# One hand-written order for the stages ahead of the typed projection in a graph, mixing and MoE kernel

## The chip, the cores and the metric

The kernel runs on one core of a Trainium2 chip. Its engines are TensorE (PE, with PEld for the loading of weights), VectorE (DVE), ScalarE (ACT), GpSimd (POOL) and SyncE (SP), each with an instruction queue of its own that it works through in order. DMAs are issued from the queues of SP, ACT and POOL; indirect DMAs (a gather or scatter of rows by a list of indices) from POOL's. The metric is the device time of one execution in microseconds (us), lower is better. Profile and timed runs are separate executions.

## What is computed

N = 3125 nodes with 256 features, E = 103125 edges sorted by receiver (`dst`), 19 node types, and a mixture of 16 experts. Everything is float32. Cut to what matters:

```python
xn = layernorm(x)                                       # per node
# graph part: linear maps by node type, attention over edges, both directions
K, Q, V = (typed_linear(xn, W, b, node_type) for W, b in ((Wk, bk), (Wq, bq), (Wv, bv)))
e0, e1, e2 = (cos(log(t + 1) * w_time + b_time) for t in edge_attr[:, :3].T)
att, v = edge_msgs(K[row], Q[col], V[row], e1, e2)      # 4 heads
agg = segment_sum([v * segment_softmax(att, col), e0], col) + the same with row and col exchanged
g = layernorm(typed_linear([agg, agg], Wa, ba) + xn) * gamma[node_type] + beta[node_type]
# mix part: linear attention over all nodes, 8 heads
q, k = elu(xn @ wq + bq) + 1, elu(xn @ wk + bk) + 1;  vm = xn @ wv + bv
kv, k_sum = sum over nodes of k^T vm, and of k
mix = ((q @ kv) / (q . k_sum + 1e-6)) @ wo + bo
x = x + g + mix
# MoE: 16 experts, the best 2 for each node, two-layer networks with relu
out = x + layernorm(xl + moe(xl)) * gamma2 + beta2      # xl = layernorm(x)
```

Since `q.sum` over heads is all that the graph attention needs of Q, the four 56-wide parts of Wq are added together ("folded") to one before the projection.

## The kernel before

Nodes lie in NT = 25 tiles of 128 rows (the last has 53). The stages ahead of the edges ("the head") are these; line numbers are those of the profile.

- **Rows of the edge list.** The receivers (`idx`, 128 x 808 and one more) are turned to float (`nf`) and written to `ends` in DRAM, 512 rows of 202. For each node tile one VectorE instruction (L391) counts how many of the 512 first entries lie below the node, which gives the row its edges begin in (`row_i`); POOL gathers that row for each of the 128 nodes (`er`, L357, one indirect DMA a tile, six buffers), and a second instruction (L401) counts within it. Both together give `start`, the place of the node's first edge, and by differences `deg`, how many it has.
- **Types' sort** (`sorted_rows`, L293 and around): a place for each node in a list sorted by type, with each type padded to whole tiles, JS = 43 of them; `stype` is that place.
- **Norms** (L424 to L430): moments by tile, a square root for each group of six tiles, then `XN` (normalised rows), whose two halves are transposed by TensorE (`pt`, L285) and copied to `XNT` by ACT (L286). POOL scatters each tile of `XN` to `xbuf` in the order of types (L351, 25 scatters, each `issue_after` the last gather of `er`).
- **Receivers' sort** (L439 to L492): nodes sorted by their number of edges, so that blocks of 128 have about the same. A matrix `pick` (25 x 64 flags a partition), running sums (`running`, L292 and L293), ranks by matmuls (L487, L488), then `place_i`. POOL scatters 25 tiles of records to `order` (L351) and loads them back as `ordt` (L555).
- **Edges** (L500 to L517): in four parts, load senders and three times, ACT takes logarithms, and a store writes records to `recs`.
- **Weights**: SP loads b, Wk, Wv, and Wq type by type (19 pieces of two loads, two buffers `wq`); VectorE folds each (L527 to L529).
- **Attention's sums** (L573 to L591): for each tile keys and values, `ps_kv` = two matmuls of 128 x 512 over `XNT`; VectorE adds biases (`k` L576, `low` L578, `v` L581), ACT takes an exponential (L579), VectorE ends `k` (L583), and TensorE adds k^T v over all tiles in `acc` (L585). The masked result is `state`.

The order of all this is not the text's: a scheduler places the instructions of the head on each engine by their readiness and its own costs. From the projection on the order is written by hand (`tc.manual_schedule()`): for each of the JS tiles `load_tile` (SP), `turn_tile`, `project` (TensorE L726; VectorE adds the bias into `prow`, L734, three buffers), pieces of the mix part (`mix`, with `queries` for four tiles at a time, L768 to L773, which need `XNT`, and `mixes`, which need `state`), and `place`, which has POOL copy the places (L739) and scatter the projected rows to `table` (L740). At tile 8 `ordered()` reads `ordt`, and the lists of edges are then worked off between tiles. Edge blocks, output and MoE follow.

The pools of the head lie on a stack: `ep` (side right) until the end of the attention's sums, `normed` (XN) inside it until the receivers' sort is done, `wqp` for the Wq pieces, and `mixs` (k, low, v) on the room that `normed` gave back.

Of the kernel before, what the change touches and what calls it, by code (L numbers as in the profile page):

```python
# [97 lines left out]
def gnn_mix_moe_kernel(ctx: ExitStack, tc: tile.TileContext, a, out):  # L98
# [97 lines left out]
    e2 = right.enter_context(tc.tile_pool(name="eprep2", bufs=2, side="right"))  # L196
# [19 lines left out]
    turned = first.enter_context(tc.tile_pool(name="turned", bufs=1))  # L216
    normed = ExitStack()
# [18 lines left out]
    for i, k in enumerate(("wq", "wk", "wv")):  # L236
        nc.sync.dma_start(wqkv[:, :, i, :], a[f"L0_mix_{k}"].rearrange("(c p) o -> p c o", p=P))
    wo = mw.tile([P, 2, D], F32, name="wo")
    nc.sync.dma_start(wo, a["L0_mix_wo"].rearrange("(c p) o -> p c o", p=P))
# [7 lines left out]
    nc.vector.tensor_scalar(bq1, bqc, 1.0, None, op0=OP.add)  # L247
# [8 lines left out]

    zp = first.enter_context(tc.tile_pool(name="zero", bufs=1))
    none = ep.tile([P, ROW], F32, name="none")
    nc.gpsimd.memset(none, -1.0)
# [3 lines left out]
    scales = zp.tile([T, 2, DZ], F32, name="scales")  # L263
# [4 lines left out]
    bo = zp.tile([T, D], F32, name="bo")  # L268
    src = a["L0_mix_bo"]
    nc.gpsimd.dma_start(bo, bass.AP(tensor=src.tensor, offset=src.offset, ap=[[0, T], [1, D]]))  # L270
    nc.vector.tensor_tensor(scales[:, 1, :D], scales[:, 1, :D], bo, OP.add)
# [4 lines left out]

    wp = first.enter_context(tc.tile_pool(name="wproj", bufs=1))
    w = wp.tile([P, T, 2, WC], F32, name="w")
# [17 lines left out]

    def sorted_rows(gp, ps_r, pick, K, J):

# [7 lines left out]
        nc.tensor.matmul(total.rearrange("p t e -> p (t e)"), ones, pv, start=True, stop=True)  # L306
        run = gp.tile([P, NT + 1, K], F32, name="run0")
# [59 lines left out]

    nf = ep.tile([P, EW + 1], F32, name="nf")
    nc.vector.tensor_copy(nf, idx)
    kept_ends = nc.gpsimd.dma_start(ends.rearrange("(p r) t -> p (r t)", p=P), nf[:, :EW]).ins  # L370
    with tc.issue_after(kept_ends):
        nc.sync.dma_start(xbuf.rearrange("(t p) d -> p t d", p=P), bc(blank, 1, JS + 1))
    down = ep.tile([P, EW], F32, name="down")
    nc.vector.tensor_tensor(down, nf[:, :EW], nf[:, 1:], OP.is_gt)
    nc.vector.tensor_reduce(bad[:, 0:1], down, AX.X, OP.max)


    ps = ps_c.tile([P, LR, P], F32, name="ps_first")
    for r in range(LR):
        nc.tensor.transpose(ps[:, r, :], nf[:, r * ET:r * ET + 1].to_broadcast([P, P]), ident)  # L380
    firsts = ep.tile([P, LR * P], F32, name="firsts")
    nc.scalar.copy(firsts, ps.rearrange("p r q -> p (r q)"))
    node_i = ep.tile([P, NT], I32, name="node_i")
    nc.gpsimd.iota(node_i, pattern=[[P, NT]], base=0, channel_multiplier=1)
    rec = ep.tile([P, NT, 4], F32, name="rec")
    node = rec[:, :, 0]
    nc.vector.tensor_copy(node, node_i)
    row = ep.tile([P, NT], F32, name="row")
    for t in range(NT):
        junk = e2.tile([P, max(ET, LR * P)], F32, name="junk", bufs=1)  # L390
        nc.vector.tensor_scalar(junk[:, :LR * P], firsts, node[:, t:t + 1], 0.0, op0=OP.is_lt, op1=OP.add,  # L391
                                accum_out=row[:, t:t + 1])
    nc.vector.tensor_scalar(row, row, -1.0, 0.0, op0=OP.add, op1=OP.max)
    row_i = ep.tile([P, NT], I32, name="row_i")
    nc.vector.tensor_copy(row_i, row)
    within = ep.tile([P, NT], F32, name="within")
    for t in range(NT):
        er = e2.tile([P, ET], F32, name="er", bufs=6)
        counted = gather_rows(er, ends, row_i[:, t:t + 1]).ins
# [20 lines left out]
    with tc.tile_pool(name="ps_t", bufs=2, space=PSUM) as ps_t:  # L420
        for g0, gn in groups:
# [7 lines left out]
            for t in range(g0, g0 + gn):  # L429
# [3 lines left out]
                with tc.issue_after(counted):  # L433
                    scatter_rows(xbuf, stype[:, t:t + 1], XN[:, t, :], "xrows")
# [1298 lines left out]
```

## Time and profile before

| What | us |
|---|---|
| median of 3 timed runs (2707.68 to 2709.11) | 2709.07 |
| the profiled execution, and its span | 2717.76, 2716.0 |
| start of the first projection matmul (L726) | 237.44 |
| er gathers, xbuf scatters, order scatters (POOL) | 52.4 to 86.7, 87.0 to 118.7, 155.1 to 187.1 |
| counts of rows (L391) | 25.7 to 51.1 |
| norms (L430), first and last start | 20.1 and 104.6 |
| first k (L576), last matmul into acc (L585) | 140.4, 227.7 |
| state done, ordt's load issued | 228.6, 190.5 |

The profiled execution is 0.3% above the median of the timed runs. Times in the text are from the start of its span. In lists of groups each row has the busy time, the mean in ns of one, and after the second bar how long the engine stood idle just before these instructions and who released it ("issue": nothing that the profile shows; "remote": a source that it doesn't know). A window row has the busy time and count of PE, PEld, DVE, ACT and POOL in turn, then the TensorE clock that was granted (1 is full), the share of DMA time and GB/s. In the timeline a row has its start, its duration, the engine (a trailing q: its queue, which issues DMAs), line, operation, tiles and, in brackets, the idle time before it.

### The profile page before, as it was taken

How to read it: one execution, taken by the hardware profiler on the slowest of the kernel's cores; microseconds unless marked ns; L12 is line 12 of the kernel's file. 1: busy time of each engine (PE TensorE's matmuls, PEld its weight loads, DVE VectorE, ACT ScalarE, POOL GpSimd, SP SyncE). 2: the span in 40 equal slices, each digit the busy share in tenths (PEclk: the TensorE clock that was granted, in tenths of full speed). 3: DMA queues.
4: the chain of work that ended last, by engine and by line, in shares of the span. 5: the costliest groups of instructions: out<-in, count | busy, mean ns of one | idle time of the engine just before them, and what ended most of it. 6: DMA issues, size and time to landing. Idle time of an engine off the chain costs nothing. (4 is left out here: it accounts for less than half of the span.)

```text
span 2716.0 us, 28309 instructions
## 1 busy us (share of the span) xinstructions
PE 2084.6 (77%) x7139; PEld 1274.6 (47%) x7139; DVE 1918.1 (71%) x3769; ACT 1230.2 (45%) x3019; POOL 1497.5 (55%) x1525
## 2 busy tenths in 40 slices
PE   2268665278898898989988888898877853599994
PEld 1034342134555455555554554455554541377773
DVE  7465777377889899999999998999972463122226
ACT  1112222265666666666666566657632350133332
POOL 3531468776777777777777776766613614222210
PEclk7579787677989898999899899898986755699997
DMA  9434567896667666666666766666636561255554
GB/s 282 137 77 129 165 194 226 286 314 183 181 202 202 177 192 192 195 197 193 190 198 202 199 187 178 192 182 188 178 124 204 174 197 66 99 174 173 174 156 146
DMA packets 236151, 496.03 MB, mean 183 GB/s; under 512 B 31509, under 2 KB 148340, under 8 KB 235476
## 3 DMA queue, kind: packets, MB, share of 16 engines
q0 software_dynamic: 88480, 325.71, 40.2%
q1 hardware_dynamic: 139428, 158.87, 20.0%
q10 hardware_dynamic: 8080, 9.59, 1.2%
q8 instruction: 63, 1.03, 0.1%
q14 instruction: 100, 0.82, 0.1%
HBM read 415.68 MB, written 78.37 MB: 182 GB/s over the span
## 5 line engine op out<-in xcount | busy, mean ns | idle before, releaser
L357 POOL DMA_INDIRECT rowt<-table,idx x854 | 999.8, 1171 | 394.6 <-issue 231.3
L1394 PE MATMUL pl<-rowt,ident 128*128 128x448 f32 (+2 forms) x944 | 496.9, 681 | 100.5 <-issue 55.3
L1394 PEld LDWEIGHTS pl<-rowt,ident 128*128 128x128 f32 x944 | 210.3, 234 | 382.2 <-issue 283.8
L1446 PE MATMUL pa<-keep,ident 128*128 128x256 f32 x1708 | 380.6, 380 | 7.0 <-DVE keep L1444 7.0
L1446 PEld LDWEIGHTS pa<-keep,ident 128*128 128x128 f32 x1708 | 325.7, 191 | 73.5 <-issue 27.7
L1359 PE MATMUL ps_u<-wide,turned 49*128 49x448 f32 (+2 forms) x708 | 323.2, 592 | 47.9 <-ACT turned L1352 27.0
L1338 DVE TENSOR_TENSOR rowt<-rowt 128x1260 f32<-128x1260 f32 (+2 forms) x118 | 178.4, 1512 | 140.4 <-DMA rowt<-table,idx 61.7
L1328 ACT ACTIVATE rowt<-rowt,KT 128x60 f32<-128x60 f32 x854 | 216.2, 334 | 20.9 <-DMA rowt<-table,idx 20.0
L1359 PEld LDWEIGHTS ps_u<-wide,turned 49*128 49x128 f32 x708 | 128.0, 194 | 189.7 <-issue 126.0
L351 POOL DMA_INDIRECT ybuf<-y,to_i x64 | 61.4, 960 | 265.0 <-DVE y L1169 224.0
L1352 ACT COPY turned<-pt 42x128 f32<-42x128 f32 (+2 forms) x118 | 30.6, 259 | 386.6 <-PE pt L1350 218.3
L1387 DVE TENSOR_TENSOR rowt<-rowt,qq 128x672 f32<-128x672 f32 (+2 forms) x236 | 197.7, 878 | 4.0
L1361 ACT ACTIVATE half<-ps_u 128x448 f32<-128x448 f32 (+2 forms) x354 | 190.9, 539 | 2.2 <-remote 1.1
L1161 ACT ACTIVATE hT<-ps_h,b 128x128 f32<-128x128 f32 x256 | 94.1, 368 | 213.2 <-PE ps_h L1160 211.5
L1160 PE MATMUL ps_h<-zT,w 128*128 128x128 f32 x1024 | 180.1, 295 | 12.6 <-ACT hT L1161 10.0
L1339 DVE TENSOR_REDUCE KT<-rowt 128x21 f32<-128x1260 f32 (+2 forms) x118 | 178.3, 1511 | 4.1
L1160 PEld LDWEIGHTS ps_h<-zT,w 128*128 128x128 f32 x1024 | 149.8, 192 | 58.2 <-ACT hT L1161 44.0
L1440 DVE TENSOR_TENSOR keep<-keep,both 128x1176 f32<-128x1176 f32 (+2 forms) x118 | 167.0, 1416 | 0.0
L1355 ACT COPY keep<-rowt 128x1344 f32<-128x1344 f32 (+2 forms) x118 | 159.1, 1348 | 13.3 <-PE pa L1446 13.3
L1165 PE MATMUL ps_e<-w,hT 128*128 x512 | 157.6, 390 | 0.0
L1373 PE MATMUL pe<-te,ident 128*128 128x256 f32 x472 | 117.1, 371 | 34.9 <-ACT te L1362 24.4
L1362 ACT ACTIVATE te<-half 128x448 f32<-128x448 f32 (+2 forms) x236 | 139.1, 590 | 7.8 <-ACT half L1361 0.3
(374 smaller groups left out, 3375.6 us busy)
## 6 DMA issues: line engine op xcount, KB each, us to landing
w<-in_L_ffn_w_dram SPq DMA_DIRECT2D x80, 512.0 KB
rowt<-table,idx POOLq DMA_INDIRECT x854
h<-in_L_gnn_Wa_dram SPq DMA_DIRECT2D x19, 512.0 KB
bias<-bbuf SPq DMA_DIRECT2D x43, 220.0 KB
zbuf<-zero SPq DMA_DIRECT2D x1, 8514.0 KB
zr<-zbuf SPq DMA_DIRECT2D x64, 129.0 KB
yb<-ybuf SPq DMA_DIRECT2D x16, 384.0 KB
xbuf<-blank SPq DMA_DIRECT2D x1, 5654.0 KB
```

The costliest lines, as they stand in the source:

```text
L357: return nc.gpsimd.indirect_dma_start(out=dst, out_offset=None, in_=buf[:, :], in_offset=IndirectOffsetOnAxis(ap=idx, axis=0))
L1160: nc.tensor.matmul(ps[:, f, :], w1[:, c, f * P:(f + 1) * P], zT[:, c, :], start=(c == 0), stop=(c == 1))
L1328: nc.scalar.activation(key[:, s, :], key[:, s, :], AF.Square, bias=chk[q]["b"]["k"][:, s0 + s, 1:2])
L1338: nc.vector.tensor_tensor(times, times, bc(rowt[:, :n, :CAP], 2, 3), OP.mult)
L1339: nc.vector.tensor_reduce(b["times"][:, s0:s1, 1::2], times, AX.X, OP.add)
L1355: nc.scalar.copy(keep[:, :n, :PROJ], rowt[:, :n, VC:QC])
L1359: nc.tensor.matmul(ps[:, :n * 2 * TD], lT, wide[:, k, :n * 2 * TD], start=True, stop=True)
L1361: nc.scalar.activation(half[:, :n, :].rearrange("p s j -> p (s j)"), ps[:, :n * 2 * TD], AF.Sin)
L1387: nc.vector.tensor_tensor(to, kt, bc(qq[:, :n, d, :], 2, 3), OP.mult)
L1394: nc.tensor.matmul(pl[:, :n], ident, part[:, :, :, a, :], start=(a == 0), stop=(a == PARTS - 1))
L1440: nc.vector.tensor_tensor(v3, v3, bc(b["both"][:, s0:s1, :3], 3, DK), OP.mult)
L1446: nc.tensor.matmul(b["pa"], ident, keep[:, s, :], start=(s0 + s == 0), stop=(s0 + s == c - 1))
```

## The change

The whole head is put under `tc.manual_schedule()`, so each engine now runs its instructions in the order of the text, and the text is rewritten to that end:

- Order: moments of the first group, `nf`, the types' `pick` and its matmuls, then all 25 row counts one after the other (`rows_of_edges`, called from inside `sorted_rows`), the first six gathers of `er`, the rest of the types' sort, the fold of b, all other moments and one square root for all tiles, edges 0 and 1. Then one loop over the 25 tiles: the gather for tile t+6, norm and transposes of t, the count within for t, and after every second tile from the fourth one `keys()`. `keys()` begins a tile of the attention's sums (`keys_of`) and ends the one before (`sum_keys`).
- Behind the loop come the 25 xbuf scatters, edges 2 and 3, and the receivers' sort as a generator, `order_rows`, cut into 14 steps, with a `keys()` behind the work of each step and one fold behind every third. Then the 25 order scatters, `ordt`, the last folds, `state` and the checks on the edge order (`down`) and times (`top`).
- Wq comes in five pieces of up to four types, and a fold is three instructions for all types of its piece.
- Each xbuf and order scatter takes its indices from a copy made by POOL (`apart`, three buffers).
- Queues: bk, bv and bq are loaded on POOL's queue, edges 0 and 1 on SP's, `gbuf` and `bbuf` stored on ACT's; Wk and Wv follow the fill of `xbuf` on SP, which no longer waits until `ends` is issued.
- Pools: `mixs` is open from the start, so the sums over keys need no room from `XN`; `early` (zq: edges, biases, and what is written first) closes before `late` (Wq pieces, receivers' sort) opens in its place; one PSUM tile `ps_c` serves three uses, and `pr` has two buffers.

What is removed is the same work in the text of before, printed above; of the new text, the lines that the prediction speaks of:

```diff
-    none = ep.tile([P, ROW], F32, name="none")
-    nc.gpsimd.memset(none, -1.0)
...
+    early = ExitStack()
+    zq = early.enter_context(tc.tile_pool(name="early", bufs=2))
+    none = zq.tile([P, ROW], F32, name="none", bufs=1)
...
-    nc.vector.tensor_tensor(scales[:, 1, :D], scales[:, 1, :D], bo, OP.add)
+    nc.gpsimd.dma_start(b[:, :PROJ], a["L0_gnn_bk"])
+    nc.gpsimd.dma_start(b[:, PROJ:2 * PROJ], a["L0_gnn_bv"])
+    bq = zq.tile([T, PROJ], F32, name="bq", bufs=1)
+    nc.gpsimd.dma_start(bq, a["L0_gnn_bq"])
...
-    for q in range(4):
-        ri = e2.tile([P, QT], I32, name="ri")
-        raw = e2.tile([P, QT, 5], F32, name="raw")
+    edges, kept_er = {}, {}
...
+    def load_edges(q, eng):
+        ri = zq.tile([P, QT], I32, name="ri")
+        raw = zq.tile([P, QT, 5], F32, name="raw")
...
+        load_rows(eng, ri, a["src"], E, EW, q * QT, (q + 1) * QT)
+        load_rows(eng, raw.rearrange("p t c -> p (t c)"), a["edge_attr_5"], 5 * E, 5 * EW, 5 * q * QT, 5 * (q + 1) * QT)
+        edges[q] = ri, raw
...
+    def keep_edges(q):
+        ri, raw = edges.pop(q)
+        rc = zq.tile([P, QT, 4], F32, name="rc")
...
         nc.scalar.dma_start(recs[:P * EW, :].rearrange("(p t) c -> p t c", t=EW)[:, q * QT:(q + 1) * QT, :], rc)
...
+    def apart(idx, side):
+        at = ep.tile([P, 1], I32, name=f"at_{side}", bufs=3)
+        nc.gpsimd.tensor_copy(at, idx)
+        return at
...
+    with tc.manual_schedule():
+        for i, k in enumerate(("w_time", "b_time")):
+            s = a[f"L0_gnn_{k}"]
+            nc.scalar.dma_start(wb[:, i, :], bass.AP(tensor=s.tensor, offset=s.offset, ap=[[0, P], [1, TD]]))
+        for q in range(2):
+            load_edges(q, nc.sync)
+        for i, k in enumerate(("wq", "wk", "wv")):
+            nc.sync.dma_start(wqkv[:, :, i, :], a[f"L0_mix_{k}"].rearrange("(c p) o -> p c o", p=P))
+        nc.sync.dma_start(wo, a["L0_mix_wo"].rearrange("(c p) o -> p c o", p=P))
+        nc.sync.dma_start(xbuf.rearrange("(t p) d -> p t d", p=P), bc(blank, 1, JS + 1))
+        load_w(w[:, :, :, :PROJ], a["L0_gnn_Wk"], nc.sync)
+        load_w(w[:, :, :, PROJ:2 * PROJ], a["L0_gnn_Wv"], nc.sync)
+        node_i = ep.tile([P, NT], I32, name="node_i")
+        nc.gpsimd.iota(node_i, pattern=[[P, NT]], base=0, channel_multiplier=1)
+        moments_of(0)
...
+        nc.vector.tensor_copy(nf, idx)
+        nc.gpsimd.dma_start(ends.rearrange("(p r) t -> p (r t)", p=P), nf[:, :EW])
...
+        nc.scalar.copy(firsts, ps.rearrange("p r q -> p (r q)"))
+        with tc.tile_pool(name="sort", bufs=1, side="right") as gp, tc.tile_pool(name="ps_r", bufs=1, space=PSUM) as ps_r:
...
+            def rows_of_edges():
+                nc.vector.tensor_copy(node, node_i)
+                for t in range(NT):
+                    junk = er_p.tile([P, max(ET, LR * P)], F32, name="junk", bufs=1)
+                    nc.vector.tensor_scalar(junk[:, :LR * P], firsts, node[:, t:t + 1], 0.0, op0=OP.is_lt, op1=OP.add,
+                                            accum_out=row[:, t:t + 1])
+                nc.vector.tensor_scalar(row, row, -1.0, 0.0, op0=OP.add, op1=OP.max)
+                nc.vector.tensor_copy(row_i, row)
+            base, own = sorted_rows(gp, ps_r, pick, T, JS, rows_of_edges)
...
+            for t in range(6):
+                kept_er[t] = er_p.tile([P, ET], F32, name="er")
+                gather_rows(kept_er[t], ends, row_i[:, t:t + 1])
...
+        nc.vector.tensor_tensor(scales[:, 1, :D], scales[:, 1, :D], bo, OP.add)
+        fold(b[:, 2 * PROJ:], bq)
+        nc.scalar.dma_start(gbuf, scales.rearrange("t i d -> t (i d)"))
+        nc.scalar.dma_start(bbuf, b)
+        for g in range(1, len(groups)):
+            moments_of(g)
...
+        nc.scalar.activation(rs, mv[:, :, 1], AF.Sqrt, bias=eps_c)
...
+        def keys_of(t):
+            ps = ps_kv.tile([P, 512], F32, name="ps_kv")
+            for c in range(2):
...
+        def sum_keys(t):
+            k, low, v = made.pop(t)
+            n = rows[t]
+            nc.vector.scalar_tensor_tensor(k, k, 1.0, low, op0=OP.add, op1=OP.max)
+            for c in range(2):
...
+        n_keys = [0]
+        def keys():
+            t = n_keys[0]
+            n_keys[0] += 1
+            if t < NTR:
+                keys_of(t)
+            if 0 < t <= NTR:
+                sum_keys(t - 1)
...
+        keep_edges(0)
+        load_edges(2, nc.scalar)
+        keep_edges(1)
+        load_edges(3, nc.scalar)
+        with tc.tile_pool(name="ps_t", bufs=2, space=PSUM, side="right") as ps_t:
+            for t in range(NT):
+                if t + 6 < NT:
+                    kept_er[t + 6] = er_p.tile([P, ET], F32, name="er")
+                    gather_rows(kept_er[t + 6], ends, row_i[:, t + 6:t + 7])
+                nc.vector.tensor_scalar(XN[:, t, :D], XN[:, t, :D], mv[:, t, 0:1], rs[:, t:t + 1],
+                                        op0=OP.subtract, op1=OP.mult)
+                transposed(XNT[:, :, t * P:(t + 1) * P], XN[:, t, :D], ps_t, "pt")
+                junk = er_p.tile([P, max(ET, LR * P)], F32, name="junk", bufs=1)
+                nc.vector.tensor_scalar(junk[:, :ET], kept_er.pop(t), node[:, t:t + 1], 0.0, op0=OP.is_lt, op1=OP.add,
+                                        accum_out=within[:, t:t + 1])
+                if t % 2 == 1 and t > 2:
+                    keys()
+        for t in range(NT):
+            scatter_rows(xbuf, apart(stype[:, t:t + 1], "x"), XN[:, t, :], "xrows")
+        normed.close()
+        for q in range(2, 4):
+            keep_edges(q)
+        early.close()
...
+        late = ExitStack()
+        gp = late.enter_context(tc.tile_pool(name="dsort", bufs=1))
+        wqp = late.enter_context(tc.tile_pool(name="wq", bufs=2))
+        step = 4
+        folds = []
+        for k in range(0, T, step):
+            n = min(step, T - k)
+            folds.append((k, n))
+        wqs = {}
+        def load_fold(i):
+            k, n = folds[i]
+            wqs[i] = wqp.tile([P, step, 2, PROJ], F32, name="wq")
+            load_w(wqs[i][:, :n], a["L0_gnn_Wq"][k:k + n], nc.sync)
+        def fold_one(i):
+            k, n = folds[i]
+            fold(w[:, k:k + n, :, 2 * PROJ:].rearrange("p t c o -> p (t c) o"),
+                 wqs.pop(i)[:, :n].rearrange("p t c o -> p (t c) o"))
+            if i + 2 < len(folds):
+                load_fold(i + 2)
+        for i in range(2):
+            load_fold(i)
...
+        def order_rows():
+            start = ep.tile([P, NT + 1], F32, name="start")
...
+            nc.tensor.matmul(ps, shift[:, 1, :], start[:, 1:], start=False, stop=True)
+            yield
...
+            dst, at = gp.tile([P, NT + 1, K], F32, name="run"), 1
+            while at <= NT:
+                nc.vector.tensor_copy(dst[:, :at], run[:, :at])
+                nc.vector.tensor_tensor(dst[:, at:], run[:, at:], run[:, :NT + 1 - at], OP.add)
+                run, dst, at = dst, run, 2 * at
+                yield
...
+        with tc.tile_pool(name="ps_d", bufs=2, space=PSUM, side="right") as ps_d:
+            steps = order_rows()
+            i = 0
+            for s, _ in enumerate(steps):
+                if n_keys[0] <= NTR:
+                    keys()
+                if s % 3 == 2 and i < len(folds):
+                    fold_one(i)
+                    i += 1
+        for t in range(NT):
+            scatter_rows(order, apart(place_i[:, t:t + 1], "o"), rec[:, t, :], "order")
+        nc.gpsimd.dma_start(ordt, order.rearrange("(t p) c -> p t c", p=P))
+        while n_keys[0] <= NTR:
+            keys()
+        while i < len(folds):
+            fold_one(i)
+            i += 1
...
+        down = nf[:, 1:]
+        nc.vector.tensor_tensor(idx[:, :EW], nf[:, :EW], down, OP.is_gt)
+        nc.vector.tensor_reduce(row_i[:, 0:1], idx[:, :EW], AX.X, OP.max)
...
+        mix_ps.close()
+        late.close()
+        right.close()
```

## The prediction

> **What bounds the kernel now.** I read the page first (span 2716.0 us; TensorE busy 77%, but in the first four slices 2, 2, 6, 8 tenths with the clock at 7, 5, 7, 9), because the change touches only what lies before the projection. Then the windows of that head, up to the first projection matmul (L726) at 237.44 us:
>
> ```profile
> core 0: us, PE busy (x) PEld busy (x) DVE busy (x) ACT busy (x) POOL busy (x), PEclk, DMA share, GB/s
> 0.00:42.00 42.00, 11.92 (x28) 5.77 (x28) 30.46 (x118) 8.74 (x14) 8.98 (x26) 0.88 0.98 276
> 42.00:100.00 58.00, 11.23 (x34) 4.94 (x34) 32.73 (x134) 7.42 (x21) 33.93 (x36) 0.52 0.79 227
> 100.00:140.00 40.00, 10.57 (x18) 4.40 (x18) 19.75 (x49) 5.76 (x10) 14.39 (x15) 0.50 0.35 115
> 140.00:200.00 60.00, 39.17 (x109) 19.11 (x109) 35.00 (x138) 8.25 (x17) 26.34 (x26) 0.80 0.32 65
> 200.00:237.00 37.00, 31.62 (x109) 15.72 (x107) 20.77 (x60) 7.00 (x18) 0.00 (x0) 0.91 0.20 52
> ```
>
> No engine fills the head: VectorE works 139 of 237 us, TensorE 105, POOL 84. It is a chain of waits. Which ones, the groups of instructions in 20 to 237 us show:
>
> ```profile
> L573 PE MATMUL ps_kv<-wqkv,XNT 128*128 128x512 f32 x100 | 53.8, 660 | 2.2 <-DVE v L581 1.4 <-DVE w L529 0.7
> L351 POOL DMA_INDIRECT order<-rec,place_i x25 | 24.7, 989 | 43.7 <-DVE w L527 36.4 <-issue 7.3
> L351 POOL DMA_INDIRECT xbuf<-XN,stype x25 | 24.4, 975 | 7.6 <-issue 7.0 <-DVE run L292 0.3 <-DMA xbuf<-XN,stype 0.3
> L391 DVE TENSOR_SCALAR_CACHE_REDUCE junk<-firsts,rec 128x512 f32<-128x512 f32 x25 | 18.4, 735 | 0.0
> L430 DVE TENSOR_SCALAR XN<-XN,mv_x,r_x 128x256 f32<-128x256 f32 x25 | 10.6, 434 | 3.2 <-remote 3.2
> L576 DVE TENSOR_TENSOR k<-ps_kv,bkv 128x256 f32<-128x256 f32 x25 | 10.6, 423 | 25.6 <-remote 20.1 <-PE ps_kv L573 5.1 <-issue 0.5
> L401 DVE TENSOR_SCALAR_CACHE_REDUCE junk<-er,rec 128x202 f32<-128x202 f32 x25 | 10.5, 419 | 20.2 <-DMA er<-ends,row_i 6.3 <-DVE XN L430 5.0 <-remote 4.9
> L527 DVE TENSOR_TENSOR w<-wq 128x112 f32<-128x112 f32 x19 | 5.1, 270 | 0.9 <-issue 0.5 <-DMA wq<-in_L_gnn_Wq_dram 0.5
> L487 PE MATMUL pr<-pick,before 128*128 128x512 f32 (+1 forms) x8 | 5.6, 796 | 5.7 <-DVE pick L470 4.1 <-DVE at L490 1.6
> L488 PE MATMUL pr<-run,ones 128*128 128x512 f32 (+1 forms) x8 | 4.5, 652 | 10.0 <-DVE run L292 10.0
> ```
>
> The reader should see that the sums over keys (L573 to L585) begin only after 140 us (first k at 140.4) although the norms (L430) are done at 104.6, and that POOL's three trains of 25 indirect DMAs (52 to 87, 87 to 119, 155 to 187 us) stand one behind the other. Last, SP's queue and the end of the head in the timeline:
>
> ```profile
> 22.96 0.37 SPq L372 DMA_DIRECT2D xbuf<-blank  x1
> 23.98 17.62 SPq L532 DMA_DIRECT2D b<-in_L_gnn_bk_dram  x1
> 53.53 13.28 SPq L523 DMA_DIRECT2D w<-in_L_gnn_Wv_dram  x2
> 66.86 9.26 SPq L523 DMA_DIRECT2D wq<-in_L_gnn_Wq_dram  x4
> ...
> 230.82 3.78 PE L768 MATMUL ps_q<-XNT,wqkv 128*128 128x512 f32 x4 [2.81 <-DVE qT L773]
> 237.44 1.74 PE L726 MATMUL ps<-w,xT 128*128 x4 [0.57 <-issue]
> ```
>
> The DMA engines are full until about 80 us, and a transfer behind them holds its queue: the 14 KB load of b took 17.62 us to issue.
>
> **The change, term by term.** All times are from the span's start. Code after the first projection tile is the same, so what counts is when that stage starts and how freely it runs.
>
> 1. *Start of the tile loop: 72 us.* Counts (25 x 0.735 = 18.4 us), types' sort (some 11) and the moments of 19 tiles (19 x 0.40) run back to back from about 19, so VectorE could be at the norms by 57. But ACT's queue now holds, ahead of its first XNT copy, the loads of edges 2 and 3 and the store of edges 1, and by the built program their issues wait for completion slots that the xbuf fill, Wk and Wv used last. So ACT, in order, stands until Wv has landed; each transpose's PSUM tile waits behind it, and VectorE behind that (its reduction over edges 1 needs ACT's logarithms). Bytes up to there: x 3.2, dst 0.4, edges 0 and 1 1.4, mix weights 1.05, xbuf fill 5.8, Wk and Wv 7.5, small ones 1.3: 20.6 MB. The first 15 us moved 238 GB/s = 3.6 MB; the other 17 MB at 297 GB/s (window 15 to 42) take 57 us: 72. Bounds: 57 (nothing held) and 76 (SP through with its last full-queue issue in before).
>
> 2. *Loop: 63 us.* Four tiles alone (4 x 1.5), then 11 pairs, each with one keys(). TensorE in order: two transposed tiles 2 x 0.38, ps_kv 1.88, acc 0.61 (full clock); acc waits for k, low, v, k, 0.42 + 0.31 + 0.42 + 0.42 = 1.57 us on VectorE: 4.8, with the XNT copy (0.37) 5.2. 11 x 5.2 = 57. Bounds: VectorE alone, 2 x (0.41 + 0.50) + 1.57 = 3.4 each; half clock (ps_kv 3.78, as L768 shows for this shape) 7.9. I take 5.2: TensorE is busy 3.25 of 5.2 us, nearest to the window 140 to 200 (39.2 of 60, clock 0.80), not to 42 to 140 (21.8 of 98, clock 0.5). End 135. The er gathers, now issued six ahead of the counts, have 15 us each and cost nothing; if the loop were faster than 1.26 us a tile, their pace in before, they would set it.
>
> 3. *Edges 2 and 3: 5.6 us.* ACT table load 1.28, two sets of logarithms 2 x 1.77, a reduction 0.77; nothing lies beside it on VectorE: 141.
>
> 4. *Fourteen steps: 67 us.* Each has a keys(): 1.57 on VectorE, then acc + next ps_kv, 0.61 + 1.88, beside which the step's own VectorE work lies: sort about 22 us and folds. The folds were 19 x (0.27 + 0.27 + 0.20) = 14 us and become five of four types; by a 128x440 add of 0.62 (L734) that is 5 x (0.62 + 0.62 + 0.35) = 8. 30/14 = 2.1 fits under 2.49. So 14 x 4.06 = 57, and the ranks' matmuls in TensorE's order 5.6 + 4.5 = 10. End 208. Bounds: 54 (VectorE alone, 22 + 24 + 8) and 102 (half clock, 14 x 6.6 + 10).
>
> 5. *To the first L726: 12 us*: state 1.2, the 9.4 us that before took from state to L726 (228.0 to 237.4), and 1.5 for the checks over edge order (two passes of about 1 us, moved from the start to here). 219.7, or 17.7 us earlier than 237.4.
>
> 6. *VectorE against POOL: +5.* xbuf's scatters come only behind the last er gather (about 120) and each has a POOL copy before it whose buffer waits for the scatter three back: 0.97 + 0.3 + 0.2 = 1.5 us, 37 us a train against 32. They lie beside loop and steps. In before VectorE stood with its inputs there, releaser unnamed ("remote"), 3.2 + 1.2 us during xbuf's train and 20.1 us (longest 11.8) around the order train. I charge the xbuf row: 4.4 x 37/32 = 5. Bounds 0 and 23 a train.
> The Trainium skill, "SBUF — State Buffer", section "SBUF: two separate sides", speaks against the change: VectorE and GpSimd share a port pair as an exclusive lock, and the loser stands for the whole instruction. By it each scatter could cost up to its own length, an estimate of 24 us a train, and the sum would end about 19 us later; the xbuf train of this trace shows far less, the order train nearly that.
>
> 7. *POOL's tail: +4.* place_i is known at 206, so the order scatters run 206 to about 248 with four writes of projected rows between them; in before they ended at 187 and ordt was issued at 190.5. With three prow buffers the tile 3 add waits for place(0), about 239, against 235 by before's spacing (239.2 to 253.0); tiles 4 to 6 are up to 8 late, then the stage has slack on every engine. Bounds 0 and 15. ordt lands near 252, before ordered() needs it (277 in before, so some 262). The Wq loads, three ahead of need, hide under the steps; uncovered, two of 1.5 MB would cost 10.
>
> The loads of bk, bv, bq on POOL, gbuf and bbuf on ACT, and the single Sqrt cost nothing: POOL has no indirect DMA until 38 us, and ACT waits anyway.
>
> Sum: 17.7 - 5 - 4 = about 9 us gained. The profiled execution took 2717.76 (span 2716.0 and 1.8 around it), 8.7 above the median 2709.07; against the first 2709, against the median 2700.
>
> **Rivals.** *A, early:* ACT isn't held (loop from 57, -15) and VectorE sets the loop (11 x 1.8 = -20) and part of the steps (-10): 2655 to 2690. For it: VectorE has only 139 us of work here. Against: the queue that took 17.62 us for 14 KB. *B, paced elsewhere:* projection tiles come at the pace of POOL's writes, and the earlier start is handed back whole: 2709. For it: L739 to L740 gaps of 1 to 2 us; against: POOL idles 45 us ahead of it. *C, slower:* VectorE stands beside both long trains as it did beside the order train, 20.1 x 37/32 = 23 us each, the second now over the first projection tiles rather than over keys. 46 - 17.7 + 4 = +32: 2741. It decides from 14 us of standing in all; at half the price 2718.
>
> **How the numbers follow.** My forecast (2690 to 2707, most likely 2700) has 0.40, A 0.20, B 0.09, C 0.31. About 0.2%, 5.4 us, is what a measurement of this kernel can tell from no change, so 2703.7 and 2714.5 part the classes: faster 0.30 + 0.20 + 0.02 = 0.52; same 0.10 of mine and 0.07 of B; slower 0.31. Range 2657 to 2730: all of mine and of B, A but its end, C up to two thirds of its price.
>
> **What would show it.** First XNT copy of tile 0 near 72 (1); last L430's counterpart near 135 and clock above 0.8 (2); place_i near 206 (4); first projection matmul near 220 to 225 (5, 6); order scatters until about 248 and the add of tile 3 late by some 4 us (7). The prediction is wrong if ACT copies before 62, if TensorE stays at half clock through the steps, or if VectorE has tens of us of unnamed waits beside the scatters.

## The result, and the profile after

The change makes the kernel slower: 2736.96 us median of 7 runs (2725.5 to 2740.64) against 2709.11 of 7 runs of before on the same chip; the ratio is 1.0092, 95% interval 1.0063 to 1.0122. The profiled execution took 2737.92 (span 2735.9), 20 more than that of before. On a second chip the same pair stands at 1.0179 (1.0142 to 1.0215), and once more there at 1.0165 (1.0138 to 1.0193). Both kernels are faster on that chip, but before gains more (2663 to 2665 us instead of 2709) than the changed kernel (2709 to 2711 instead of 2737); where that comes from is followed further down.

The windows of the changed kernel, cut as before's were, and one more (busy us and count of PE, PEld, DVE, ACT, POOL, then the clock, DMA share, GB/s):

```profile
0.00:42.00 42.00, 4.41 (x8) 1.89 (x8) 30.90 (x101) 1.87 (x2) 13.52 (x31) 0.75 1.02 274
42.00:100.00 58.00, 13.37 (x38) 6.08 (x38) 32.31 (x123) 11.81 (x22) 10.63 (x12) 0.59 0.76 218
100.00:140.00 40.00, 26.64 (x90) 12.26 (x90) 20.83 (x77) 9.25 (x24) 21.50 (x31) 0.91 0.18 57
140.00:200.00 60.00, 35.55 (x98) 16.64 (x99) 37.62 (x102) 10.60 (x19) 22.15 (x31) 0.83 0.36 113
200.00:237.00 37.00, 25.86 (x73) 12.73 (x72) 21.16 (x56) 4.17 (x10) 10.92 (x20) 0.86 0.29 56
237.00:300.00 63.00, 40.35 (x157) 25.37 (x157) 26.76 (x106) 8.36 (x22) 31.59 (x52) 0.84 0.58 148
```

TensorE now works from 100 us on at a granted clock of 0.83 to 0.91, where before had 0.50 until 140: the sums over keys do run between the norms. But in 200 to 237 POOL is at work (10.9 us; nothing in before), and in 237 to 300, the first tiles of the projection, VectorE is busy 27 of 63 us. The groups of the changed kernel say what for, the first six in 15 to 300 us, the last two in 180 to 620:

```profile
L502 PE MATMUL ps_kv<-wqkv,XNT 128*128 128x512 f32 x100 | 60.4, 737 | 0.0
L354 POOL DMA_INDIRECT xbuf<-XN,at_x x25 | 26.2, 1050 | 6.9 <-POOL at_x L426 5.6 <-issue 1.1 <-DVE k L505 0.3
L505 DVE TENSOR_TENSOR k<-ps_kv,bkv 128x256 f32<-128x256 f32 x25 | 10.6, 424 | 54.8 <-PE ps_kv L502 53.5 <-issue 1.3
L542 DVE TENSOR_SCALAR XN<-XN,mv_x,r_x 128x256 f32<-128x256 f32 x25 | 10.1, 402 | 0.0
L376 DVE TENSOR_TENSOR w<-wq 128x448 f32<-128x448 f32 (+1 forms) x5 | 3.0, 593 | 0.0
L638 PE MATMUL pr<-pick,before 128*128 128x512 f32 (+1 forms) x8 | 3.4, 507 | 0.0
...
L830 DVE TENSOR_TENSOR prow<-ps,bias 128x440 f32<-128x440 f32 x43 | 26.3, 611 | 48.4 <-DMA table<-prow,to 24.0 <-PE ps L822 19.3 <-issue 5.1
L354 POOL DMA_INDIRECT order<-rec,at_o x25 | 24.5, 979 | 7.2 <-issue 3.8 <-POOL at_o L426 3.3 <-POOL to L835 0.2
```

The same add in before, in 180 to 620 us:

```profile
L734 DVE TENSOR_TENSOR prow<-ps,bias 128x440 f32<-128x440 f32 x43 | 26.3, 611 | 27.8 <-PE ps L726 25.9 <-issue 1.9
```

The L830 row decides. The bias add of a projected tile, which in before waited for TensorE (25.9 of 27.8 us, the rest without a named cause), now also waits 24.0 us for the write of an earlier tile's rows to land, so that one of the three `prow` buffers comes free. The timeline of POOL shows why that write is late, and VectorE's what it holds:

```profile
251.94 0.19 POOL L426 COPY at_o<-place_i 128x1 int32<-128x1 int32 x1
252.41 0.98 POOL L354 DMA_INDIRECT order<-rec,at_o  x1 [0.28 <-issue]
253.69 0.96 POOL L836 DMA_INDIRECT table<-prow,to  x1 [0.30 <-issue]
254.66 0.19 POOL L426 COPY at_o<-place_i 128x1 int32<-128x1 int32 x1
...
266.38 0.98 POOL L354 DMA_INDIRECT order<-rec,at_o  x1 [0.28 <-issue]
273.86 1.61 POOL L666 DMA_DIRECT2D ordt<-order  x1 [6.50 <-issue]
275.95 1.03 POOL L836 DMA_INDIRECT table<-prow,to  x1 [0.28 <-POOL to L835]
```

```profile
240.50 0.62 DVE L830 TENSOR_TENSOR prow<-ps,bias 128x440 f32<-128x440 f32 x1 [0.73 <-PE ps L822]
256.91 0.62 DVE L830 TENSOR_TENSOR prow<-ps,bias 128x440 f32<-128x440 f32 x1 [7.11 <-DMA table<-prow,to]
264.13 0.62 DVE L830 TENSOR_TENSOR prow<-ps,bias 128x440 f32<-128x440 f32 x1 [4.62 <-DMA table<-prow,to]
269.51 0.62 DVE L830 TENSOR_TENSOR prow<-ps,bias 128x440 f32<-128x440 f32 x1 [3.39 <-DMA table<-prow,to]
280.96 0.62 DVE L830 TENSOR_TENSOR prow<-ps,bias 128x440 f32<-128x440 f32 x1 [8.87 <-DMA table<-prow,to]
```

Tile 0's rows, ready at 236.2, are written at 253.7, behind most of the order train (221.2 to 267.4); tile 3's own write, at 275.9, stands behind ordt's load too, which waits 6.5 us for the train to land. Two numbers sum up each run from here on: the *first* bias add, which shows how long the head took, and the time from the first to the last, which shows how freely the projection ran (below, "the stage"). With the time at which place_i is known they are the marks of a run. Before has 239.2 and 264.0, the changed kernel 235.6 and 285.2: 3.6 us won, 21.2 lost. The last add is 17.7 later, the span 19.9.

### The profile page after: what moved, and what is told of

Its sections match the earlier page's. It is cut to its first block, busy times and chain, and to the rows that moved or that the text cites. A ratio compares the mean times of both kernels' runs of the same rounds, so it can differ in the third digit from the quotient of the medians.

```text
span 2735.9 us, 28265 instructions
## 1 busy us (share of the span) xinstructions
PE 2083.7 (76%) x7139; PEld 1274.3 (47%) x7139; DVE 1921.0 (70%) x3724; ACT 1229.5 (45%) x3016; POOL 1532.5 (56%) x1577
## 4 chain that ended last, share of the span: by engine, by line
PE 38%; DVE 19%; issue 18%; DMA 8%; POOL 7%; ACT 6%; SPq 2%; another core or an unknown queue 1%; ACTq 0%; POOLq 0%; DVEq 0%
PE pl L1490 12%; PE pa L1542 10%; PE ps_u L1455 6%; POOL rowt L360 3%; POOL ybuf L354 2%; PE pe L1469 2%; DMA rowt<-table,idx 2%; PE ps_kv L502 2%; DVE KT L1435 2%; DVE rowt L1434 2%; ACT rowt L1424 1%; PE ps_yo L1066 1%; DVE rowt L1483 1%; ACT keep L1451 1%; SPq L372 1%
## 5 line engine op out<-in xcount | busy, mean ns | idle before, releaser
L360 POOL DMA_INDIRECT rowt<-table,idx x854 | 1020.5, 1195 | 379.8 <-issue 234.3
L1542 PEld LDWEIGHTS pa<-keep,ident 128*128 128x128 f32 x1708 | 325.8, 191 | 74.0 <-issue 27.8
L1434 DVE TENSOR_TENSOR rowt<-rowt 128x1260 f32<-128x1260 f32 (+2 forms) x118 | 178.5, 1513 | 148.0 <-ACT rowt L1425 86.4
```

Source lines behind the costliest of these rows:

```text
L360: return nc.gpsimd.indirect_dma_start(out=dst, out_offset=None, in_=buf[:, :], in_offset=IndirectOffsetOnAxis(ap=idx, axis=0))
L1434: nc.vector.tensor_tensor(times, times, bc(rowt[:, :n, :CAP], 2, 3), OP.mult)
L1542: nc.tensor.matmul(b["pa"], ident, keep[:, s, :], start=(s0 + s == 0), stop=(s0 + s == c - 1))
```

## The experiments

Every version is an edit of the changed kernel. The rows of before and of the changed kernel on the second kind of chip are fresh profiles. The chips fall in two kinds by what before takes: 2709 to 2722 (the first kind, as the first chip) or some 2665 (the second kind); ratios are compared within a kind only. The first four versions ran on another chip of the second kind than the changed kernel did, and the changed kernel was not run beside the versions of the first kind. Times are us in the profiled execution. The ratios of the single edits have intervals that overlap the changed kernel's, save that of the doubled train; for them the marks carry the verdict.

| version, kind of chip | place_i | first add | first to last add | ratio to before (95%) |
|---|---|---|---|---|
| before, 1st (the first chip) | 154.6 | 239.2 | 264.0 | 1 |
| changed, 1st (the first chip) | 220.4 | 235.6 | 285.2 | 1.0092 (1.0063 to 1.0122) |
| before, 2nd | 136.6 | 205.7 | 268.3 | 0.9985 (0.9964 to 1.0006) |
| before, 2nd, again | 135.6 | 204.6 | 267.7 | 0.9995 (0.9972 to 1.0018) |
| changed, 2nd | 223.1 | 236.7 | 287.6 | 1.0179 (1.0142 to 1.0215) |
| changed, 2nd, again | 224.0 | 239.2 | 284.7 | 1.0165 (1.0138 to 1.0193) |
| six prow buffers, 2nd | 224.9 | 240.2 | 275.7 | 1.0141 (1.0106 to 1.0177) |
| order train twice, 2nd | 220.5 | 234.8 | 316.5 | 1.0272 (1.0232 to 1.0312) |
| sort ahead of keys, 2nd | 196.5 | 238.0 | 265.4 | 1.0120 (1.0083 to 1.0158) |
| edges on SP, 2nd | 209.1 | 224.3 | 285.8 | 1.0146 (1.0109 to 1.0183) |
| sums one later, 2nd | 205.1 | 220.5 | 284.6 | 1.0112 (1.0077 to 1.0147) |
| first combination, 2nd | 178.5 | 208.5 | 277.4 | 1.0041 (1.0015 to 1.0066) |
| 25 index buffers, 1st | 224.5 | 240.0 | 277.4 | 1.0040 (1.0009 to 1.0070) |
| no keys in the loop, 1st | 202.3 | 260.7 | 264.9 | 1.0079 (1.0048 to 1.0111) |
| second combination, 1st | 171.0 | 208.7 | 270.4 | 0.9910 (0.9874 to 0.9947) |
| the same, 25 index buffers, 1st | 176.1 | 216.7 | 270.6 | 0.9894 (0.9846 to 0.9941) |
| third combination, 2nd | 157.6 | 196.7 | 267.2 | 0.9960 (0.9943 to 0.9977) |

**Is it the train ahead of the writes?** Three versions took away the shortage of buffers, doubled the train, and moved it forward.

Six buffers:

```diff
-            prow = mp.tile([P, WC], F32, name="prow", bufs=3)
+            prow = mp.tile([P, WC], F32, name="prow", bufs=6)
```

> Six buffers for the projected rows instead of three; nothing else. Theory (tail): in the changed kernel the writes of projected rows stand in POOL's queue behind the order scatters, and VectorE waits 24.0 us for buffers at tiles 3 to 6; with six it goes on until tile 6, which then waits for the first write (issued at 253.7, landed near 257), and ordered() waits for ordt, near 277: 10 to 18 us less, 2719 to 2727, wait of the bias add on the write of rows below 8 us. Rival (pace elsewhere): the waits are a symptom, the stage has another pace: 2733 to 2741.

In 150 to 620 us of this version:

```profile
L830 DVE TENSOR_TENSOR prow<-ps,bias 128x440 f32<-128x440 f32 x43 | 26.3, 612 | 33.2 <-PE ps L822 33.1
L704 DVE CAST ord_i<-ordt 128x25 int32<-128x25 f32 x3 | 0.4, 177 | 6.9 <-DMA ordt<-order 6.9
```

The waits on writes are gone and the stage takes 275.7 instead of 285 to 288. The rest of the loss stays: `ordered()` runs at 287.4, after 6.9 us of waiting for ordt, whose load is issued at 279.9. So the buffers are one way in which the train holds the stage, ordt is the other. The stage gained 9 to 12 us and the time 6 to 10 (1.0141 against 1.0165 and 1.0179, with overlapping intervals): the low end of what was expected, and less.

The train twice:

```diff
-        for t in range(NT):
+        for t in (*range(NT), *range(NT)):
             scatter_rows(order, apart(place_i[:, t:t + 1], "o"), rec[:, t, :], "order")
```

> The order scatters are issued twice (the second set writes the same rows), so POOL's train ahead of the first write of rows is doubled. Theory (tail): 25 more at 1.45 to 1.85 us each, all on the path: +36 to +46, 2773 to 2783, the add of tile 3 near 295 to 303. Rival (the loss arises in the head or behind the projection): the train is covered by other work and less than +15 shows: below 2752.

The stage grows to 316.5, 29 to 32 more than in the changed kernel. The head is no longer (first add 234.8). The theory's sign holds; its size was too high, and the place is three tiles further on. The writes of tiles 0 to 2 are let in between the scatters, so tile 3's add comes at 257.4, much as in the changed kernel (256.9), and it is tile 6's that waits longest, 17.85 us, until 289.6. The waits on writes add up to 34.7 us, as the group of the bias add in 150 to 620 us of this version shows:

```profile
L830 DVE TENSOR_TENSOR prow<-ps,bias 128x440 f32<-128x440 f32 x43 | 26.3, 612 | 61.8 <-DMA table<-prow,to 34.7 <-PE ps L822 25.2 <-PE ps_xt L286 1.1
```

The train forward:

```diff
-                if n_keys[0] <= NTR:
+                if s % 2 == 1 and n_keys[0] <= NTR:
                     keys()
```

> A keys() behind every second step of the receivers' sort instead of every step; the seven keys() left follow the order scatters in the text, so VectorE and TensorE do them while POOL scatters. Theory (tail): place_i at about 200 (153 + 7 x 4.8 + 7 x 2) instead of 220, train over by about 246, state near 230 (8 later than now), so the first tiles find POOL free: tile 6's add near 266 instead of 281: 2718 to 2727. Rival (what counts is when state and the first projection matmul come): they come 5 to 10 later, 2742 to 2748.

place_i comes at 196.5, the train is over at 235.6, and the stage takes 265.4, no longer than in before. The same row in the same stretch:

```profile
L830 DVE TENSOR_TENSOR prow<-ps,bias 128x440 f32<-128x440 f32 x43 | 26.3, 611 | 29.6 <-PE ps L822 29.6
```

No wait on a write is left, and state and the first add come no later (238.0), against the rival: seven keys() without sort steps between them run at 3.94 us each. Yet on this chip the version is still 1.2% behind before. What is left lies in the head.

**What makes the head long?** First ACT's queue. In the changed kernel:

```profile
66.84 0.96 ACTq L203 DMA_DIRECT2D raw<-in_edge_attr_dram  x2
74.35 0.23 ACTq L207 DMA_DIRECT2D raw<-in_edge_attr_dram  x1
74.62 1.74 ACT L413 ACTIVATE rc<-raw,ones 128x202 f32<-128x202 f32 x3 [10.28 <-DMA raw<-in_edge_attr_dram]
80.36 1.14 ACTq L203 DMA_DIRECT2D ri<-in_src_dram  x2
82.45 0.65 ACT L287 COPY XNT<-pt 128x256 f32<-128x256 f32 x2 [6.09 <-DMA ri<-in_src_dram]
```

```diff
-        load_edges(2, nc.scalar)
+        load_edges(2, nc.sync)
...
-        load_edges(3, nc.scalar)
+        load_edges(3, nc.sync)
```

> Edges 2 and 3 are loaded on SP's queue behind Wv, not on ACT's. Theory (ACT held): ACT no longer stands in its queue from 66.8 to 74.4 and 79.9 to 82.4; first norm near 68 instead of 78.4 and every mark up to place_i 8 to 12 earlier, all of it kept: 2725 to 2730. Rival (the head's start is not what ends last, or the logarithms wait for their data anyway): below 3 us, 2734 to 2740.

With the loads on SP's queue nothing parts the logarithms of edges 0 and 1 (the trace of that version):

```profile
63.12 1.74 ACT L413 ACTIVATE rc<-raw,ones 128x202 f32<-128x202 f32 x3
64.89 0.37 ACTq L415 DMA_DIRECT2D recs<-rc  x1
65.31 1.75 ACT L413 ACTIVATE rc<-raw,ones 128x202 f32<-128x202 f32 x3 [0.45 <-ACT rc L413]
```

The first norm comes at 69.1, and the first add 12.4 to 14.9 us earlier than in the changed kernel on chips of this kind, with the stage as long as ever (285.8). ACT was held. The time falls by less than the marks, 5 to 9 us (1.0146).

Then the chain through VectorE in each keys():

```diff
+        def end_keys(t):
+            k, low, v = made[t]
+            nc.vector.scalar_tensor_tensor(k, k, 1.0, low, op0=OP.add, op1=OP.max)
...
             if 0 < t <= NTR:
-                sum_keys(t - 1)
+                end_keys(t - 1)
+            if 1 < t <= NTR + 1:
+                sum_keys(t - 2)
```

> The changed kernel with each tile's sum into acc put one keys() later, so TensorE never stands on the four VectorE instructions ahead of it (1.57 us a tile; four buffers for k and v). Theory (that chain is a term of loop and steps): 11 x 1.5 less in the loop, some 14 x 1.2 in the steps; place_i near 190 instead of 220, first projection matmul near 203, the order train as long as now: 25 to 30 faster than the changed kernel. Rival (the chain is not what paces them; VectorE is, or the clock falls as TensorE idles more): below 8.

First add 220.5, 16 to 19 earlier, and by the ratios 14 to 18 us in all, where 25 to 30 were forecast. The loop takes as long as it did (first to last norm 64 us, as in the changed kernel beside it), and all of the gain is in the steps, from first key behind the loop to place_i 49.8 instead of 66.3. So the theory holds for the steps. In the loop another ring (a circle of waits) remains, as the order in this version's trace shows: ps_kv (123.53 us), the four VectorE instructions (from 125.45), the norms of the next two tiles behind them (126.78, 127.45), their transposes, and ps_kv again (128.25): 4.72 us, and the changed kernel's shortest rounds take as long.

**Where does before's advantage come from?** Before and the changed kernel were profiled on one chip of the second kind, twice.

> The kernel before once more, unchanged, profiled beside the next ones on one chip. In the first four experiments the chip ran it in 2665 where the first chip took 2709, and a version whose last bias add (503.4) comes when before's does (503.2) took 1.2% more. Theory (tail, nothing else): the ratio is 1.000, and from the last bias add to the end it takes as long as the changed kernel, within 5. Rival (something behind the projection, too, got slower): before needs 15 to 30 less from the last bias add to the end.

> The changed kernel once more, unchanged, on the same chip. Theory (tail): last bias add 15 to 20 later than in before, and the whole 15 to 25 (0.6 to 0.9%) slower. Rival (also behind the projection): 35 to 50 slower (1.4 to 1.9%) on this chip, of which only 15 to 20 ahead of the last bias add.

> Before once more, profiled on the chip of the next two. Theory (unnamed waits lengthen before's head on some chips): where before takes some 2710 to 2722 its last bias add is near 503 and VectorE has over 20 of unnamed waits ahead of 240; where it takes 2665, near 474 and none. Rival (chance of one execution): the waits and the time don't go together.

> The changed kernel on the same chip. Theory: it has no such waits on either kind of chip, as its scatters run beside chains that stand on TensorE, and its last bias add is at 520 to 525 on both: 1.0 to 1.1% slower than a before with the waits, 1.7 to 1.8% slower than one without. Rival: the ratio is the same on both.

In the changed kernel the last add comes 50 to 52 us later than in before there, which none of the forecasts for the first pair had. The part behind the last add is not slower: 2185 for before and 2178 for the changed kernel in one pair, 2178 and 2185 in the other (span less last add). The stage is 17 to 19 us slower, and the head 31 to 35: before's first add comes at 205.7 and 204.6 there, where it came at 239.2 on the first chip. The L576 row of before on that chip, in 20 to 237 us:

```profile
L576 DVE TENSOR_TENSOR k<-ps_kv,bkv 128x256 f32<-128x256 f32 x25 | 10.5, 421 | 4.5 <-PE ps_kv L573 4.5
```

On the first chip this row had 25.6 us of idle time, 20.1 of them unnamed ("remote" in the rows). In all, VectorE had 31.5 us of unnamed waits before 240 there (20.1 on k, 4.9 on the counts, 3.3 on `over`, 3.2 on the norms); on the second kind it has none, its waits called "issue" fall from 13.6 to 0.3 us, and the last add is 29.2 and 30.9 us earlier. The changed kernel has none on either kind, and its first adds are alike (235.6, 236.7, 239.2). So the 237 us that the prediction counted from held some 30 us that before's order waits on the first kind of chip and not on the second, and that the changed kernel doesn't wait on either. Three later versions without keys in the loop show such waits on a chip of the first kind as well (VectorE 5.5, 2.1 and 8.3 us, ACT 7.0, 7.5 and 22.3), so they are not tied to before's program. What they are was not tried.

**Do the causes, taken away together, make the hand order pay?** Edges on SP, sums one later, and a keys() at every second step:

> Three edits to the changed kernel together: edges 2 and 3 on SP's queue, a keys() only behind every second step of the receivers' sort, and the sums one keys() later. Theory: head start -11, place_i near 165, train over by 212 beside the last keys, first projection matmul near 190, no waits of the bias add on writes: 45 to 55 faster than the changed kernel, 20 to 35 faster than before by the marks up to the last bias add. Rival (a loss behind the projection that the marks don't show): no faster than before although its last bias add comes 30 earlier.

First add 208.5, close to before's 205, but the train (179 to 223) still ran into the stage: tile 3's add waits 10.7 us for a write, the stage takes 277.4, and the version is 0.4% slower than before. Neither theory had it right: nothing is lost behind the projection, and the train was not early enough.

More room between scatters and their landing, alone, on a chip of the first kind:

```diff
-        at = ep.tile([P, 1], I32, name=f"at_{side}", bufs=3)
+        at = ep.tile([P, 1], I32, name=f"at_{side}", bufs=25)
```

> 25 buffers instead of three for POOL's copies of the indices: a scatter no longer waits for the landing of the one three back. Theory (the train's pace is part of the tail): the order train takes 25 x 1.45 = 36 us and three writes, instead of 46, tile 6's add comes 7 to 9 earlier: 0.3% below the changed kernel's 1.0179 of before (1.0140 to 1.0155). Rival (the engines move the data no faster, only the wait goes elsewhere, to ordt's load): below 0.1%.

The train with its three writes took 37 us (225.5 to 262.6) instead of 46, the waits on writes 17.0 instead of 24.0, and the stage 277.4. The ratio, 1.0040, lies 0.5% below that of the changed kernel on the first chip, where the ends of the two intervals just overlap. The first add is 4.4 us later here, so the last one comes only 3.4 earlier.

No keys in the tile loop:

```diff
-                if t % 2 == 1 and t > 2:
-                    keys()
```

> The changed kernel without the keys() in the tile loop: 14 run in the steps, 11 behind the order scatters. Theory (tail): the loop falls to POOL's pace for er, 25 x 1.27 = 32 us instead of 63, place_i comes near 190 and the train is over by 235; the 11 keys at 4.0 us each put state at about 235, 10 later than now, yet the last bias add comes near 505 to 510 instead of 524: ratio to before 1.010 to 1.014. Rival (the start of the projection decides): 10 us slower, 1.020 or more.

The loop falls to 32 us, as expected (79.2 to 111.7), but place_i is at 202.3, not 190: behind the loop VectorE and ACT need 23 us for edges 2 and 3 and the first key, and 14 steps take 68 as ever. The first add, 260.7, is 25 us later than the changed kernel's on the first chip, the stage is down to 264.9, and the whole is 1.0079, which the intervals don't part from the changed kernel's 1.0092: what the tail gives back the head takes.

The same together with edges on SP and sums one later, and once more with 25 index buffers:

> Three edits: no keys() in the tile loop, edges 2 and 3 on SP's queue, sums one keys() later. Theory: loop from 69 to 101, steps at VectorE's pace (1.57 + 2.1 = 3.7 each, 52), place_i near 155, train over near 200 while 11 keys at 2.2 us run; state near 182, first projection matmul near 192 and no wait on writes: last bias add near 463, 11 earlier than in before: 0.995 to 0.998 of before. Rival (VectorE and POOL get in each other's way, or the clock falls): place_i near 170 and no faster than before, 1.000 to 1.006.

> As the one before, and 25 buffers for the copies of indices. Theory: with the train behind keys, its pace is hidden: within 0.1% of the one before. Rival (the train still decides): 0.3% faster than that.

On a chip of the first kind both beat before, 0.9910 and 0.9894. How much of that is before's own unnamed waits is open, since before was not profiled beside them. The two versions' difference is within the intervals, so no effect of the train's pace shows any more. place_i came at 171 and 176, later than hoped: VectorE stood from 103.7 to 113.6 in the first of them, for ACT came to the logarithms of edges 2 and 3 only at 111.8, behind its copies of XNT. So these went into the loop:

```diff
+                if t in (12, 18):
+                    keep_edges(2 if t == 12 else 3)
...
-        for q in range(2, 4):
-            keep_edges(q)
```

> No keys() in the tile loop, edges 2 and 3 on SP's queue and kept inside the loop (at tiles 12 and 18) instead of behind it, sums one keys() later. In the version without this last edit VectorE stood from 103 to 116 for the edges. Theory: place_i near 160, state near 185, first projection matmul near 196, last bias add near 467: 0.3 to 0.5% faster than before where before has no unnamed waits, 1.2 to 1.5% where it has. Rival (the order train or VectorE in the steps decides): no earlier than 479, as without this edit.

On a chip of the second kind, where before has no unnamed waits, this third combination takes 0.9960 of its time (0.9943 to 0.9977), 2652.78 against 2663.03: faster than both kernels. No version without the last edit ran on this kind, so what that edit adds by itself is not shown. Two windows of the third combination, and below them the same two of the changed kernel on this chip:

```profile
100.00:140.00 40.00, 32.33 (x85) 15.82 (x84) 32.37 (x87) 6.90 (x15) 30.76 (x38) 0.78 0.47 142
140.00:200.00 60.00, 53.42 (x186) 29.06 (x185) 42.99 (x124) 9.69 (x24) 37.96 (x61) 0.91 0.30 64
```

```profile
100.00:140.00 40.00, 27.00 (x92) 12.86 (x93) 21.40 (x80) 8.80 (x23) 19.02 (x25) 0.87 0.16 49
140.00:200.00 60.00, 35.41 (x97) 16.08 (x97) 36.02 (x99) 11.10 (x21) 24.12 (x37) 0.83 0.35 110
```

All three engines do more in 100 to 200 us: TensorE 85.8 us against 62.4, VectorE 75.4 against 57.4, POOL 68.7 against 43.1. place_i is known at 157.6, the train is over at 200, and 2.1 us of waits on writes are left.

## Why the prediction was wrong

The step that failed is the seventh, POOL's tail: it was priced at 4 us and cost 21.2. Steps 1 and 3 were too short as well, by 6 and 6.5 us. By the prediction's own steps, on the first chip:

1. *Start of the tile loop, 72:* the mechanism was right (edges on SP: first norm at 69 instead of 78 to 80), the size was 6 too small. The first norm ran at 78.4 and the first copy of XNT at 82.4; ACT was held twice, until 74.4 and again until 82.4.
2. *Loop, 63:* measured 62.7 (78.4 to 141.1). But not for the reason given: with the chain of the sums out of TensorE's way, the loop stayed at 64, so the match is in part luck.
3. *Edges 2 and 3, 5.6:* 12.1 from the end of the loop to the first key in the steps (153.2). The logarithms took 6.4; then came the sort's first small matmuls and a ps_kv of 3.76 us at a granted clock of 0.50, where 1.88 was usual in the loop; the step had not counted these.
4. *Steps, 67:* measured 67.2, and that the chain of the sums is a part of it is shown by the version with the sums one later (49.8 us). Two smaller parts made up for one another: the ranks' matmuls took 6.9 us instead of 10, and four of the ps_kv 2.9 to 3.4 us instead of 1.88.
5. *To the first projection matmul, 12:* measured 12.1. So that matmul came at 232.5 instead of 219.7, and 4.9 us were won where 17.7 were forecast.
6. *VectorE against POOL, +5:* 0. No unnamed wait of VectorE stands in the changed kernel's head on either kind of chip, so the charge was wrong. Its reading of before was off, too: during xbuf's train VectorE's unnamed waits are 2.1 and 2.8 us at the counts and 3.2 at a norm, 8.1 in all, not 4.4. The lock of the Trainium skill ("SBUF — State Buffer", "SBUF: two separate sides") doesn't show as a cost here either: the estimate of up to 24 us a train did not come, with both trains beside VectorE's work. That section ties the lock to VectorE operations in a 2-port mode, or with two SBUF inputs against a GpSimd operation that reads SBUF, a condition that the prediction left out; which operations here meet it was not tried.
7. *POOL's tail, +4, bounds 0 to 15:* 21.2, the step that failed. It had the place, the queue and the buffers right, and three things wrong. The train takes 46 us with three writes in it, not 42 with four, and starts 11 us ahead of the first projection matmul instead of 14 (at 221 instead of 206). The write of tile 3 stands behind ordt's load as well, which waits for the landing of the whole train (275.9). And "then the stage has slack on every engine" was asserted without a row: tile 6's add comes at 280.96, in before at 262.65, and that lateness (18.3 from the span's start, 22.0 from the first add) is still there at the last tile (17.7, 21.2). Tile 6's add in before:

```profile
262.65 0.62 DVE L734 TENSOR_TENSOR prow<-ps,bias 128x440 f32<-128x440 f32 x1 [0.42 <-PE ps L726]
```

At the first add 3.6 are won, 21.2 are lost in the stage and 2.2 behind it: 19.9 slower in the profile, where 17.7 won and 9 lost were forecast.

Rival C's number, 2741, is 4 from the result, but its mechanism is refuted, and the closeness is luck: in the changed kernel VectorE has no unnamed waits beside the trains. What decided was the tail that the forecast had itself priced too low. A (ACT not held) is refuted by the loads on SP, B (the start is handed back whole, to POOL's writes) was nearest in mechanism, without the further loss.

One premise failed that no step names: that the 237 us of before's head were its own length. On the second kind of chip it is some 202, and there the same change costs 1.7 to 1.8%.

## What to carry to other kernels

A hand order must be made per queue as well as per engine: a train of indirect DMAs that is put where its data is first ready stands ahead of everything later on that queue, and a small load behind it that must wait for all of it to land lengthens the stop (by 8 us here). Bringing the train's input forward (here the sort ahead of the sums) took away all of the stage's loss, more buffers for the consumer (six for `prow`) somewhat over half. A stage in which no engine is full can still be a single chain; take its lateness as kept unless a window shows where it would be made up.

## What the runs showed of the hardware that was not expected

The two kinds of chip differ in waits that have no named cause. On the first kind VectorE and ACT have them in some stretches in which POOL issues indirect DMAs one behind the other, on the second none: 31.5 us of VectorE's in before's head, and 47.6 us in the MoE stage's scatters (2130 to 2380 us), where the changed kernel on the same chip has 29.4 and both kernels have none on the second kind. From the last scaled row of the output stage to the first expert's matmul both kernels took 182 us on the first chip and 161 to 162 on the second. The longest of these waits in before's head, 11.85 us, lasted as long as twelve scatters (0.97 us each). What makes them is open. The change's cost, measured against before on one chip each time, is 0.9% or 1.7 to 1.8% by which kind of chip it is.
